# A graph layer on one core: node tiles in offset stages of four, and an output that starts as x + a s

## The chip, the cores and the metric

The kernel runs on one core of a Trainium2 chip. A core has five engines that run side by side and meet through semaphores: PE (matrix products, results in PSUM), DVE (vector), ACT (scalar functions), POOL (general, here it issues gathers) and SP (issues transfers). Sixteen DMA engines move data. The metric is device time in microseconds (us); lower is better. Five runs of the kernel before took 5407.76, 5438.72, 5442.06, 5452.63 and 5453.91 us: the median is 5442.06.

## The reference

There are 12,500 nodes with 160 values each (64 scalars, and 32 vectors of 3) and 400,000 edges, sorted by destination. A node's row is normalized and cut at zero, mapped by four small matrices (two for what is sent along edges, y, and two for what stays, s), and scaled by the node's attribute a. Each edge takes y of its source, multiplies it with weights that a two-layer network makes of the edge's 16 attributes, and adds the result to its destination. The sums z are mapped again and added:

```python
h = jnp.maximum(_layernorm(x, axis=-1), 0.0)
s0 = x0 @ W_sc0 * a * inv0;   y0 = x0 @ W_l1_0 * a * inv0     # x0, x1: the two parts of h
ys0 = y0[edge_src];  ys1 = y1[edge_src]
w = silu(edge_length_embedded @ fc_W1 * ...) @ fc_W2 * ...
z = zeros.at[edge_dst].add(mid) * inv_nb                      # mid: products of w, ys, edge_attr
o0 = z0 @ W_l2_0 * a * inv_mid
out = x + C_S * s + C_X * o
```

## The kernel before, in words

It works in four stages, in the program's order.

Index work (L93 to L152). The edges' destinations are loaded as a 128x3136 table (dst_i). DVE reduces them over windows of three edge tiles (L107), POOL over the partitions (L112), and DVE derives for each group of four windows the first node tile (tile_i), for each edge its row in the window (drel), and one flag, far_i, for edges that no window holds (POOL's second reduction, L151). The temporary tables lie in the pool "idx", which is closed before the node stage. Then the weights are loaded and scaled (L156 to L192), by transfers from ACT's queue.

Node stage (L220 to L256). 98 node tiles of 128 rows, in 14 groups of seven. SP loads a group of x (L217). Per tile: statistics on DVE (L231, L232), one root per group on ACT (L234), normalization on DVE in two pieces (L240, L242), two transposes on PE (L246, L247), the cut at zero on ACT and DVE (L249, L250), two products on PE that give y and s side by side (L252, L253), y times a to yb on ACT (L254), s to acc on DVE (L255). SP stores each group of yb to y_d in HBM (L256). The order of the instructions is left to the framework's scheduler; pools with three or four buffers set how far stages overlap.

Edge loop (L277 to L464), unrolled, with its order written out by hand. 3125 edge tiles of 128 edges, in 782 blocks of four; three blocks make a group. POOL gathers the rows of y_d for each tile (L310), up to eight blocks ahead, into ten buffers yg. PE makes the hidden layer (L319) and the weights (L341), ACT moves the weights out of PSUM (L262, L263: tile wt), DVE multiplies (L268 to L275: tile pr), PE sums the products of a window with a selection matrix (L385), and ACT copies the sums out (L390, L392). Per group PE transposes the sums (L400), maps them (L409) and places them on two node tiles (L421); DVE adds both at once to acc, at an offset from a register that it loads itself (L426, L429). L364 and L366 build the selection from drel on DVE.

After the loop every engine reads far_i (L480) and runs a slow path only if it is set, which it is not here.

Output (L558 to L566). x is loaded again, ACT scales acc by a tile by tile (L562), DVE adds it to x in two pieces, one of them with its columns reordered (L563, L565), and ACT's queue stores (L566).

Of the kernel before, what the change touches and what calls it, by code (L numbers as in the profile page):

```python
# [34 lines left out]
GN = 7  # L35
# [6 lines left out]
def kernel(  # L42
# [45 lines left out]
    nc.vector.memset(eps, EPS)  # L88

# [4 lines left out]
    nc.sync.dma_start(src_sb, src)  # L94
# [3 lines left out]
    far_i = const.tile([P, 1], I32, name="far_i")  # L98
    full = T // WT
    with tc.tile_pool(name="idx", bufs=1) as ip:  # L100
        dst_i = ip.tile([P, TP], I32, name="dst_i")
        nc.sync.dma_start(dst_i, dst)
        nc.vector.tensor_copy(drel, dst_i)
        neg = ip.tile([P, NG * GW], F32, name="neg")
# [6 lines left out]
        negb = ip.tile([P, NG * GW], F32, name="negb")  # L111
        nc.gpsimd.partition_all_reduce(negb, neg, P, bass_isa.ReduceOp.max)  # L112
        first = ip.tile([P, NG], F32, name="first")
# [36 lines left out]
        farb = ip.tile([P, 1], F32, name="farb")  # L150
        nc.gpsimd.partition_all_reduce(farb, far, P, bass_isa.ReduceOp.max)  # L151
        nc.vector.tensor_copy(far_i, farb)  # L152
# [3 lines left out]
    w1 = const.tile([P, 2 * FC_H], F32, name="w1")  # L156
    nc.vector.memset(w1, 0.0)
    for i in range(P // FC_IN):
        nc.scalar.dma_start(w1[FC_IN * i:FC_IN * (i + 1), FC_H * (i % 2):FC_H * (i % 2 + 1)], fc_w1)
    w2 = const.tile([P, NW], F32, name="w2")  # L160
    for i in range(2):
        for to, of, m in ((0, 0, M0), (M0, 2 * M0, M1), (M0 + M1, M0, M0), (2 * M0 + M1, 2 * M0 + M1, M1)):
            nc.scalar.dma_start(w2[FC_H * i:FC_H * (i + 1), to:to + m], fc_w2[:, of:of + m])
    nc.vector.tensor_scalar(w2, w2, 1.0 / math.sqrt(FC_H), None, ALU.mult)

    wn0 = const.tile([M0, 2, M0], F32, name="wn0")
    nc.scalar.dma_start(wn0[:, 0, :], w_l1_0)
    nc.scalar.dma_start(wn0[:, 1, :], w_sc0)
    nc.vector.tensor_scalar(wn0[:, 0, :], wn0[:, 0, :], 1.0 / math.sqrt(M0), None, ALU.mult)
    nc.vector.tensor_scalar(wn0[:, 1, :], wn0[:, 1, :], C_S / math.sqrt(M0), None, ALU.mult)  # L170
    wn1 = const.tile([3 * M1, 2, 3 * M1], F32, name="wn1")
    nc.vector.memset(wn1, 0.0)
    for c in range(3):
        s = slice(M1 * c, M1 * (c + 1))
        nc.scalar.dma_start(wn1[s, 0, s], w_l1_1)
        nc.scalar.dma_start(wn1[s, 1, s], w_sc1)
    nc.vector.tensor_scalar(wn1[:, 0, :], wn1[:, 0, :], 1.0 / math.sqrt(M1), None, ALU.mult)
    nc.vector.tensor_scalar(wn1[:, 1, :], wn1[:, 1, :], C_S / math.sqrt(M1), None, ALU.mult)

    wo = const.tile([P, 3, D], F32, name="wo")  # L180
    nc.vector.memset(wo, 0.0)

    def o1(c):
        return slice(M0 + M1 * c, M0 + M1 * (c + 1))

    nc.scalar.dma_start(wo[0:M0 + M1, 0, 0:M0], w_l2_0)
    for rows, k, c in ((slice(96, P), 0, 0), (slice(0, 32), 1, 1), (slice(32, 64), 1, 2)):
        nc.scalar.dma_start(wo[rows, k, o1(c)], w_l2_1[M0:, :])
    for rows, k, c in ((slice(64, P), 1, 0), (slice(0, 64), 2, 1), (slice(64, P), 2, 2)):
        nc.scalar.dma_start(wo[rows, k, o1(c)], w_l2_1[0:M0, :])  # L190
    nc.vector.tensor_scalar(wo[M0:M0 + M1, 0, 0:M0], wo[M0:M0 + M1, 0, 0:M0], 1.0 / math.sqrt(3.0), None, ALU.mult)
    nc.vector.tensor_scalar(wo, wo, C_X / math.sqrt(10.0 * (M0 + M1)), None, ALU.mult)  # L192
# [3 lines left out]
    nc.sync.dma_start(a_sb, attr)  # L196

# [15 lines left out]
    def load_x(pool, g, n):  # L213
        xt = pool.tile([P, GN, D], F32, name="xt")
        if g + n == NT and N % P:
            nc.vector.memset(xt[:, n - 1, :], 0.0)  # L216
        node_dma(g, n, lambda rows, t, p: nc.sync.dma_start(xt[:p, t, :], by_tile(x[rows, :])))  # L217
        return xt

    with (  # L220
        tc.tile_pool(name="nx", bufs=4) as nx,
        tc.tile_pool(name="nd", bufs=3) as nd,
        tc.tile_pool(name="nd_pt", bufs=3, space=PSUM) as nd_pt,
        tc.tile_pool(name="nd_po", bufs=3, space=PSUM) as nd_po,
    ):
        for g, n in groups:
            xt = load_x(nx, g, n)
            st = nd.tile([P, GN, 6], F32, name="st")
            mv = nd.tile([P, GN, 2], F32, name="mv")
            for j in range(n):  # L230
                nc.vector.bn_stats(st[:, j, :], xt[:, j, :])  # L231
                nc.vector.bn_aggr(mv[:, j, :], st[:, j, :])  # L232
            rstd = nd.tile([P, GN], F32, name="rstd")
            nc.scalar.activation(rstd[:, :n], mv[:, :n, 1], AF.Sqrt, bias=eps)  # L234
            nc.vector.reciprocal(rstd[:, :n], rstd[:, :n])
            yb = nd.tile([P, GN, D], F32, name="yb")
            for j in range(n):
                i = g + j
                h = nd.tile([P, D], F32, name="h")
                nc.vector.tensor_scalar(h[:, 0:M0], xt[:, j, 0:M0], mv[:, j, 0:1], rstd[:, j:j + 1],  # L240
                                        ALU.subtract, ALU.mult)
                nc.vector.tensor_scalar(h[:, M0:].rearrange("p (c u) -> p c u", c=3),  # L242
                                        xt[:, j, M0:].rearrange("p (u c) -> p c u", c=3),
                                        mv[:, j, 0:1], rstd[:, j:j + 1], ALU.subtract, ALU.mult)
                pt = nd_pt.tile([P, 2, P], F32, name="pt")
                nc.tensor.transpose(pt[0:M0, 0, :], h[:, 0:M0], ident)  # L246
                nc.tensor.transpose(pt[0:3 * M1, 1, :], h[:, M0:], ident)  # L247
                hT = nd.tile([P, 2, P], F32, name="hT")
                nc.scalar.activation(hT[0:M0, 0, :], pt[0:M0, 0, :], AF.Relu)  # L249
                nc.vector.tensor_scalar(hT[0:3 * M1, 1, :], pt[0:3 * M1, 1, :], 0.0, None, ALU.max)  # L250
                po = nd_po.tile([P, 2, D], F32, name="po")
                nc.tensor.matmul(po[:, :, 0:M0], hT[0:M0, 0, :], wn0, start=True, stop=True)  # L252
                nc.tensor.matmul(po[:, :, M0:], hT[0:3 * M1, 1, :], wn1, start=True, stop=True)  # L253
                nc.scalar.activation(yb[:, j, :], po[:, 0, :], AF.Copy, scale=a_sb[:, i:i + 1])  # L254
                nc.vector.tensor_copy(acc[:, i, :], po[:, 1, :])  # L255
            node_dma(g, n, lambda rows, t, p: nc.sync.dma_start(by_tile(y_d[rows, :]), yb[:p, t, :]))  # L256
# [8 lines left out]
    def multiply(pr, tmp, wt, yg, ev, n):  # L265
# [8 lines left out]
                             wt[:, :n, M0:96].unsqueeze(2).to_broadcast([P, n, 3, M1]), y1)  # L274
        nc.vector.tensor_mul(pr[:, :n, M0:96], wt[:, :n, 160:NW], tmp[:, :n, 3, :])  # L275

    with (  # L277
        tc.tile_pool(name="ld", bufs=2) as ld,
        tc.tile_pool(name="yg", bufs=10) as ygp,
        tc.tile_pool(name="hid", bufs=4) as hid,  # L280
# [328 lines left out]
```

## Time and profile before

| | us |
|---|---|
| median of five runs | 5442.06 |
| the profiled execution: its time, its span | 5432.29, 5430.4 |
| index work, until x is asked for | 0 to 47.9 |
| node stage, first statistics to last copy into acc | 52.2 to 281.7 |
| first gather, first product of the edge loop | 283.95, 292.2 |
| edge loop ends, output begins | 5377 |
| busy in the span: PE, DVE, ACT, POOL | 3773.9, 2781.8, 2592.3, 3210.4 |

The busy times are sums over stages that have different limits, so they do not tell what bounds any one of them; the stages are read one by one. A wait is given as "engine, tile and line <- releaser: us in total, times, longest", and names what was late last. "issue" and "remote" stand for a releaser that the profile does not tell. The end of a matmul is modelled, not recorded.

### The profile page before, as it was taken

To read this page: it belongs to the slowest core of one execution; us is meant where nothing else is said; L and a number is where in the kernel's file an instruction comes from. 1 tells how busy PE (TensorE), PEld (TensorE's weight loads), DVE (VectorE), ACT (ScalarE), POOL (GpSimd) and SP (SyncE) were. 2 spreads that over 40 slices of the span, in tenths; PEclk is the share of its full clock that TensorE was granted. 3 is DMA by queue.
4 is the path that set the end of the run, shared out by engine and by line. 5 is a ranking of instruction groups with operands and counts; after the bars stand their busy time and mean duration, and the time that the engine had idled before them with its cause. 6 is when DMAs were issued, how large, how long until landed. Compare 5 with 4: busy or idle time off the path is not lost. (4 is left out here: it accounts for less than half of the span.)

```text
span 5430.4 us, 60313 instructions
## 1 busy us (share of the span) xinstructions
PE 3773.9 (69%) x17263; PEld 2663.4 (49%) x17263; DVE 2781.8 (51%) x6412; ACT 2592.3 (48%) x9298; POOL 3210.4 (59%) x3135
## 2 busy tenths in 40 slices
PE   5846777777777676767666777767776776776764
PEld 3534544554555454545444555445554554554543
DVE  6634554544555554555445555545555555555455
ACT  1224454444554454545444445444454544454456
POOL 0065666656666666666566666666666666666661
PEclk9977787877778887878788788887788888888887
DMA  2122222222222222222222222222222222222224
GB/s 84 57 65 55 59 57 57 58 55 58 55 59 61 56 57 57 60 58 58 56 59 57 56 58 57 59 56 57 58 59 59 57 58 60 58 60 58 58 55 134
DMA packets 245943, 327.78 MB, mean 60 GB/s; under 512 B 66040, under 2 KB 195352, under 8 KB 245352
## 3 DMA queue, kind: packets, MB, share of 16 engines
q0 software_dynamic: 150000, 256.20, 17.7%
q1 hardware_dynamic: 81030, 59.43, 3.7%
q10 hardware_dynamic: 14578, 8.25, 0.5%
q8 instruction: 141, 2.31, 0.2%
q14 instruction: 194, 1.59, 0.1%
HBM read 307.62 MB, written 16.00 MB: 60 GB/s over the span
## 5 line engine op out<-in xcount | busy, mean ns | idle before, releaser
L310 POOL DMA_INDIRECT yg<-y_d,src_sb x3125 | 3202.5, 1025 | 2080.8 <-DVE pr L275 956.6
L385 PE MATMUL pz<-pr,sel 128*128 128x256 f32 x6250 | 1877.8, 451 | 218.9 <-issue 128.5
L385 PEld LDWEIGHTS pz<-pr,sel 128*128 128x128 f32 x6250 | 1387.5, 232 | 468.5 <-issue 162.8
L262 ACT ACTIVATE wt<-pw,ev 128x96 f32<-128x96 f32 x3125 | 810.7, 344 | 1184.2 <-issue 995.2
L271 DVE TENSOR_TENSOR pr<-wt,yg 128x256 f32<-128x256 f32 x782 | 329.9, 422 | 1601.9 <-ACT wt L263 1178.3
L390 ACT ACTIVATE zs<-pz 32x192 f32<-32x192 f32 x1042 | 337.8, 324 | 989.8 <-remote 455.3
L341 PE MATMUL pw<-w,hT 64*128 64x192 f32 x6250 | 803.2, 380 | 0.2 <-issue 0.2
L341 PEld LDWEIGHTS pw<-w,hT 64*128 64x128 f32 x6250 | 552.6, 207 | 407.2 <-issue 406.8
L392 ACT ACTIVATE zs<-pz 32x64 f32<-32x64 f32 x3126 | 669.8, 214 | 41.8
L400 PE MATMUL px<-ident,zs 128*128 128x128 f32 (+1 forms) x783 | 215.1, 352 | 516.7 <-ACT zs L390 284.7
L429 DVE TENSOR_TENSOR acc<-acc,px 128x320 f32 x261 | 127.2, 487 | 855.6 <-remote 315.8
L409 PE MATMUL px<-wo,za 128*128 128x160 f32 x1566 | 338.6, 361 | 319.2 <-issue 149.2
L421 PE MATMUL px<-os,place 128*128 128x160 f32 x1044 | 263.6, 385 | 334.9 <-ACT os L411 219.4
L270 DVE TENSOR_REDUCE tmp<-tmp 128x128 f32<-128x384 f32 x782 | 463.8, 593 | 27.0
L409 PEld LDWEIGHTS px<-wo,za 128*128 128x128 f32 x1566 | 264.6, 222 | 390.9 <-issue 187.6
L268 DVE TENSOR_TENSOR tmp<-yg,ev 128x384 f32<-128x384 f32 x782 | 431.6, 552 | 8.6 <-DMA yg<-y_d,src_sb 5.9
L273 DVE TENSOR_TENSOR pr<-wt,yg 128x384 f32<-128x384 f32 x782 | 431.6, 552 | 0.0
L400 PEld LDWEIGHTS px<-ident,zs 128*128 128x128 f32 (+1 forms) x783 | 105.7, 154 | 634.8 <-ACT zs L390 304.8
L319 PE MATMUL px<-xe,w 32*128 32x512 f32 x782 | 316.0, 698 | 128.2 <-issue 84.0
L263 ACT ACTIVATE wt<-pw 128x384 f32<-128x384 f32 x782 | 398.3, 509 | 0.0
L421 PEld LDWEIGHTS px<-os,place 128*128 128x128 f32 x1044 | 186.8, 231 | 411.5 <-ACT os L411 243.5
L366 DVE TENSOR_TENSOR sel<-sel,ev 128x1152 f32<-128x1152 f32 (+1 forms) x261 | 353.7, 1355 | 14.4 <-DMA ev<-in_e 5.4
(78 smaller groups left out, 2025.4 us busy)
## 6 DMA issues: line engine op xcount, KB each, us to landing
yg<-y_d,src_sb POOLq DMA_INDIRECT x3125
xe<-in_e SPq DMA_DIRECT2D x784, 32.0 KB
xt<-in_x SPq DMA_DIRECT2D x26, 560.0 KB
y_d<-yb SPq DMA_DIRECT2D x13, 560.0 KB
out<-xt ACTq DMA_DIRECT2D x13, 560.0 KB
ev<-in_e SPq DMA_DIRECT2D x32, 192.0 KB
src_sb<-in_src SPq DMA_DIRECT2D x1, 1568.0 KB
dst_i<-in_dst SPq DMA_DIRECT2D x1, 1568.0 KB
```

The source lines that it names most:

```text
L262: nc.scalar.activation(wt[:, k, 0:96], pw[:, k, 0:96], AF.Copy, scale=ev[:, k, 0:1])
L263: nc.scalar.activation(wt[:, :n, 96:NW], pw[:, :n, 96:NW], AF.Copy)
L268: nc.vector.tensor_tensor(tmp[:, :n, 0:3, :], y1, ev[:, :n, 1:4].unsqueeze(3).to_broadcast([P, n, 3, M1]), ALU.mult)
L270: nc.vector.tensor_reduce(tmp[:, :n, 3, :], tmp[:, :n, 0:3, :].rearrange("p t c u -> p t u c"), AX.X, ALU.add)
L273: nc.vector.tensor_mul(pr[:, :n, 96:192].rearrange("p t (c u) -> p t c u", c=3), wt[:, :n, M0:96].unsqueeze(2).to_broadcast([P, n, 3, M1]) ...
L310: nc.gpsimd.indirect_dma_start(out=yg[:, k, :], out_offset=None, in_=y_d, in_offset=bass.IndirectOffsetOnAxis(ap=src_sb[:, t:t + 1], axis=0))
L341: nc.tensor.matmul(pw[:, k, 0:NW], hT[r, o:o + P], w2[r, :], start=True, stop=True)
L366: nc.vector.tensor_tensor(sel[:, :n, 0:3, :], sel[:, :n, 3:4, :].to_broadcast([P, n, 3, WN]), ev[:, :n, 1:4].unsqueeze(3).to_broadcast([P, ...
L385: nc.tensor.matmul(pz[:, 0:PC], sels[g][:, t % TG, :, :], pr[:, k, :], start=t % WT == 0, stop=last)
L392: nc.scalar.activation(zs[:, 192 + M0 * c:192 + M0 * (c + 1)], pz[WN * c:WN * (c + 1), 192:PC], AF.Copy)
L409: nc.tensor.matmul(po[:m, :], za[:, k, :m], wo[:, k, :], start=k == 0, stop=k == 2)
L421: nc.tensor.matmul(ps[:, h, :], place[:m, h, :], os[:m, :], start=True, stop=True)
```

## The change

The node stage is cut into parts of four tiles, and its order is written out by hand for PE, ACT, DVE and SP: in one step the statistics and centering of part q, the leaving of part q-3, the maps of part q-2 and the transposes of part q-1. Only the mean is taken off, with the cut at zero, on ACT from x (h); the factor 1/deviation, times a, is the positive number ra and is applied when results leave PSUM. acc starts as x + ra times the mapped row, in the columns' own order, so that weights are laid out for that order instead. x is loaded first, stores of y_d are issued by ACT, the loads of edge weights move to SP, and the index work stands partly after part 6 (first_nodes), partly after the last part (relate). far_i comes from a PE product in place of POOL's second reduction. In the loop the sums are multiplied by a as they are added, in two instructions per group instead of one. The output stage only stores acc, from two queues in turn. Groups have eight tiles. (Lines that stand unchanged in a new function, and removed ones that are printed above, are partly left out.)

```diff
-GN = 7
+GN = 8
+HN = 4
...
+    start = ctx.enter_context(ExitStack())
+    ip = start.enter_context(tc.tile_pool(name="idx", bufs=1))
+    dst_i = ip.tile([P, TP], I32, name="dst_i")
+    neg = ip.tile([P, NG * GW], F32, name="neg")
+    negb = ip.tile([P, NG * GW], F32, name="negb")
+    def first_nodes():
+
         nc.vector.tensor_copy(drel, dst_i)
...
-        negb = ip.tile([P, NG * GW], F32, name="negb")
         nc.gpsimd.partition_all_reduce(negb, neg, P, bass_isa.ReduceOp.max)
+
+    def relate(cnt):
...
-        farb = ip.tile([P, 1], F32, name="farb")
-        nc.gpsimd.partition_all_reduce(farb, far, P, bass_isa.ReduceOp.max)
-        nc.vector.tensor_copy(far_i, farb)
+        nc.tensor.matmul(cnt, far, one, start=True, stop=True)
+        nc.vector.tensor_scalar(far_i, cnt, 1.0, None, ALU.min)
...
+    def node_weights():
+        nc.vector.memset(wnr, 0.0)
...
+        for c in range(3):
+            s = slice(M1 * c, M1 * (c + 1))
+            nc.scalar.dma_start(wnr[c::3, 0, s], w_l1_1)
...
+        nc.vector.tensor_scalar(wn1[:, 0, :], wnr[:, 0, :], 1.0 / math.sqrt(M1), None, ALU.mult)
+        nc.vector.tensor_scalar(wn1[:, 1, :].rearrange("p (u c) -> p c u", c=3),
+                                wnr[:, 1, :].rearrange("p (c u) -> p c u", c=3), C_S / math.sqrt(M1), None, ALU.mult)
...
+    def edge_weight_loads():
+        nc.gpsimd.memset(w1, 0.0)
+        for i in range(P // FC_IN):
+            nc.sync.dma_start(w1[FC_IN * i:FC_IN * (i + 1), FC_H * (i % 2):FC_H * (i % 2 + 1)], fc_w1)
...
+    def edge_weights():
+        nc.vector.tensor_scalar(w2, w2, 1.0 / math.sqrt(FC_H), None, ALU.mult)
...
+        nc.vector.tensor_scalar(wo[:, :, M0:].rearrange("p k (u c) -> p k c u", c=3),
+                                wor[:, :, M0:].rearrange("p k (c u) -> p k c u", c=3), f, None, ALU.mult)
...
-        tc.tile_pool(name="nx", bufs=4) as nx,
-        tc.tile_pool(name="nd", bufs=3) as nd,
-        tc.tile_pool(name="nd_pt", bufs=3, space=PSUM) as nd_pt,
-        tc.tile_pool(name="nd_po", bufs=3, space=PSUM) as nd_po,
+        tc.tile_pool(name="nx", bufs=5) as nx,
+        tc.tile_pool(name="ns", bufs=5) as ns,
+        tc.tile_pool(name="nd", bufs=2) as nd,
+        tc.tile_pool(name="nd_pt", bufs=2, space=PSUM) as nd_pt,
+        tc.tile_pool(name="nd_po", bufs=4, space=PSUM) as nd_po,
...
+        xts, ybs, state = {}, {}, {}
+        parts = [(g, j, min(HN, n - j)) for g, n in groups for j in range(0, n, HN)]
+
+        def load_x(g, n):
+            xt = nx.tile([P, GN, D], F32, name="xt")
+            if g + n == NT and N % P:
+                nc.gpsimd.memset(xt[:, n - 1, :], 0.0)
+            node_dma(g, n, lambda rows, t, p: nc.sync.dma_start(xt[:p, t, :], by_tile(x[rows, :])))
+            xts[g] = xt
+        def center(q):
+
+            g, j, n = parts[q]
...
+                nc.vector.bn_aggr(mv[:, k, :], st[:, k, :])
+            nm = ns.tile([P, HN], F32, name="nm")
+            nc.vector.tensor_scalar(nm[:, :n], mv[:, :n, 0], -1.0, None, ALU.mult)
+            h = nd.tile([P, HN, D], F32, name="h")
+            for k in range(n):
+                nc.scalar.activation(h[:, k, :], xt[:, j + k, :], AF.Relu, bias=nm[:, k:k + 1])
+            ra = ns.tile([P, HN], F32, name="ra")
+            nc.scalar.activation(ra[:, :n], mv[:, :n, 1], AF.Sqrt, bias=eps)
...
+        def turn_rows(q):
+            g, j, n = parts[q]
+            nc.vector.reciprocal(ra[:, :n], ra[:, :n])
+            nc.vector.tensor_mul(ra[:, :n], ra[:, :n], a_sb[:, g + j:g + j + n])
+            pt = nd_pt.tile([P, 2, HN, P], F32, name="pt")
+            for k in range(n):
+                nc.tensor.transpose(pt[0:M0, 0, k, :], h[:, k, 0:M0], ident)
+                nc.tensor.transpose(pt[0:3 * M1, 1, k, :], h[:, k, M0:], ident)
...
+        def map_rows(q):
+            hT = nd.tile([P, 2, HN, P], F32, name="hT")
+            nc.scalar.activation(hT[0:M0, 0, :n, :], pt[0:M0, 0, :n, :], AF.Copy)
+            nc.vector.tensor_copy(hT[0:3 * M1, 1, :n, :], pt[0:3 * M1, 1, :n, :])
+            for k in range(n):
                 po = nd_po.tile([P, 2, D], F32, name="po")
+                nc.tensor.matmul(po[:, :, 0:M0], hT[0:M0, 0, k, :], wn0, start=True, stop=True)
+                nc.tensor.matmul(po[:, :, M0:], hT[0:3 * M1, 1, k, :], wn1, start=True, stop=True)
...
+        def leave(q):
+            for k, po in enumerate(pos):
+                nc.scalar.activation(yb[:, j + k, :], po[:, 0, :], AF.Copy, scale=ra[:, k:k + 1])
+                nc.vector.scalar_tensor_tensor(acc[:, g + j + k, :], po[:, 1, :], ra[:, k:k + 1], xt[:, j + k, :],
+                                               op0=ALU.mult, op1=ALU.add)
+            if q + 1 == len(parts) or parts[q + 1][0] != g:
+                m = j + n
+                node_dma(g, m, lambda rows, t, p: nc.scalar.dma_start(by_tile(y_d[rows, :]), yb[:p, t, :]))
...
+        LEAD = 3
+        with tc.manual_schedule(engines={mybir.EngineType.PE, mybir.EngineType.Activation, mybir.EngineType.DVE,
+                                         mybir.EngineType.SP}):
+            for g, n in groups[:2]:
+                load_x(g, n)
+            nc.sync.dma_start(a_sb, attr)
+            node_weights()
+            nc.sync.dma_start(dst_i, dst)
+            for g, n in groups[2:LEAD]:
+                load_x(g, n)
+            nc.sync.dma_start(src_sb, src)
+            last = len(parts) - 1
+            for q in range(len(parts) + 3):
+                if q <= last and parts[q][1] == 0:
...
+                if q == min(2, last):
+                    edge_weight_loads()
+                if q == min(6, last):
+                    first_nodes()
+                if q <= last:
+                    center(q)
+                if 0 <= q - 3 <= last:
+                    leave(q - 3)
+                if 0 <= q - 2 <= last:
+                    map_rows(q - 2)
+                if 0 <= q - 1 <= last:
+                    turn_rows(q - 1)
+            pt = nd_pt.tile([P, 2, HN, P], F32, name="pt")
+            edge_weights()
+            relate(pt[0:1, 0, 0, 0:1])
+    start.close()
...
+        tc.tile_pool(name="selp", bufs=3) as selp,
+        tc.tile_pool(name="prod", bufs=3) as prod,
...
-            to = acc[:, ds(i, 2), :]
-            nc.vector.tensor_tensor(to, to, ps, ALU.add)
+            for h in range(2):
+                to = acc[:, ds(i + h, 1), :]
+                nc.vector.scalar_tensor_tensor(to, ps[:, h:h + 1, :], a_sb[:, ds(i + h, 1)], to,
+                                               op0=ALU.mult, op1=ALU.add)
...
+    for i, (g, n) in enumerate(groups):
+        eng = (nc.sync, nc.scalar)[i % 2]
+        node_dma(g, n, lambda rows, t, p: eng.dma_start(by_tile(out[rows, :]), acc[:p, g + t.start:g + t.stop, :]))
```

## The prediction

> **What bounds the kernel now.** I read the table of windows by stage first, then the timeline of the seams between stages, then one period of the edge loop, then the waits. The columns of a window are: length, busy us (and instructions) of PE, PEld, DVE, ACT and POOL, granted TensorE clock, share of the DMA engines, GB/s.
>
> ```profile
> 48.00:282.00 234.00, 197.33 (x590) 129.17 (x590) 140.16 (x604) 68.98 (x211) 0.00 (x0) 1.00 0.23 69
> ...
> 308.00:373.00 65.00, 9.80 (x31) 6.74 (x33) 7.90 (x19) 8.50 (x32) 41.29 (x43) 0.50 0.20 54
> 373.00:5340.00 4967.00, 3515.32 (x16390) 2491.78 (x16386) 2541.59 (x5631) 2446.11 (x8832) 3142.54 (x3065) 0.81 0.21 58
> ...
> 5377.00:5430.40 53.40, 0.00 (x0) 0.00 (x0) 20.87 (x30) 32.65 (x98) 0.00 (x0) 0.50 0.99 300
> ```
>
> There are four stages: the index work (0 to 48), the node stage (48 to 282), the edge loop (284 to 5377) and the output (5377 to 5430). The last is bound by the DMA engines (share 0.99), and moved this:
>
> ```profile
> DMA packets 25480, 16.04 MB, mean 303 GB/s; under 512 B 476, under 2 KB 25476, under 8 KB 25476
> ```
>
> The seams, from the timeline (start, length, engine, line):
>
> ```profile
> 47.90 16.94 SPq L217 DMA_DIRECT2D xt<-in_x  x5
> 52.24 0.55 DVE L231 BATCH_NORM_STATS2 st<-xt 128x6 f32<-128x160 f32 x2 [3.90 <-DMA xt<-in_x]
> ...
> 281.40 0.33 DVE L255 COPY acc<-po 128x160 f32<-128x160 f32 x1 [1.33 <-ACT yb L254]
> 283.95 1.30 POOL L310 DMA_INDIRECT yg<-y_d,src_sb  x1 [236.27 <-DMA xe<-in_e]
> 292.17 0.56 DVE L268 TENSOR_TENSOR tmp<-yg,ev 128x384 f32<-128x384 f32 x1 [3.68 <-DMA yg<-y_d,src_sb]
> ```
>
> x is asked for only at 47.90; 98 node tiles then take 229.5 us from the first statistics to the last copy, 2.34 each. One period of the loop:
>
> ```profile
> 1017.02 0.95 POOL L310 DMA_INDIRECT yg<-y_d,src_sb  x1 [0.30 <-issue]
> 1020.47 1.04 ACT L262 ACTIVATE wt<-pw,ev 128x96 f32<-128x96 f32 x4 [5.48 <-issue]
> 1021.92 0.42 DVE L271 TENSOR_TENSOR pr<-wt,yg 128x256 f32<-128x256 f32 x1 [9.94 <-ACT wt L263]
> 1023.07 0.29 DVE L275 TENSOR_TENSOR pr<-wt,tmp 128x128 f32<-128x128 f32 x1
> 1023.42 0.95 POOL L310 DMA_INDIRECT yg<-y_d,src_sb  x1 [5.46 <-DVE pr L275]
> 1023.61 0.49 DVE L429 TENSOR_TENSOR acc<-acc,px 128x320 f32 x1 [0.25 <-PE px L421]
> ```
>
> POOL issues gathers until all ten yg buffers are full, then waits for a product to free one; the product waits for ACT, and ACT for a PE result. The sum into acc (L429) comes after POOL has restarted. Over the loop:
>
> ```profile
> POOL yg L310 <- DVE pr L275: 956.6, 230, 11.1
> ```
>
> The sum into acc, by line (min/median/max ns):
>
> ```profile
> L429 DVEq FUSED_REGOPS  x261: 93/93/104, 375.5 to 5373.9; - x131
> L429 DVE TENSOR_TENSOR acc<-acc,px x261: 480/487/490, 379.1 to 5376.8; 128x320 f32 x131
> ```
>
> **The change, part by part.**
>
> *Start.* x is now first on SP's queue, and its buffers no longer wait for the index work. Before the first statistics DVE scales the node weights: eight ACT-queue issues at the 0.43 to 0.61 us of L167 to L176, some 5 us, and a landing like that of x (47.90 to 52.24, 4.3). PE needs ident, done at 11.48 on POOL. So the pipeline starts near 11.5 instead of 52.2.
>
> *Node period.* A part has four tiles. PE per tile: two transposes that start 0.21 apart (61.49, 61.70 on the timeline), 0.45 for the L252 pair, 0.58 for the L253 pair: 1.45, or 5.8 a part. DVE per part: statistics 4 x 0.29, four sums into acc at the 0.33 of L255, one 96x512 copy 0.6 (four times 128 elements of L250 at 0.285, less three starts), small ones 0.45: 3.5. ACT: four Relus at the 0.33 of L562, a root 0.3, four yb at 0.39, a 64x512 copy at L324's 0.60, half a store issue at 0.37: 4.0. All fit beside PE, but one chain crosses them: transposes 1.7, ACT's copy 0.8 with its signal, DVE's copy 0.7 (it follows ACT's, as L250 followed L249), a signal 0.2, the maps 4.1, less 0.4 for the first map that needs ACT's half alone: 7.1. I take 7.2 and 24.5 parts: 176. Filling (statistics 1.3, Relus 1.3, two table loads at 1.28, transposes 1.7, the next two parts' turns on ACT) costs about 8, draining 2; first_nodes puts L103 and L107 to L110 (5.3) and a 3.3 us POOL reduction, beside which L191 took 1.84, into DVE's order: 5 after slack. Last sum into acc: 11.5 + 8 + 176 + 2 + 5 = 202, against 281.7: **-80**. Ends: PE-bound, 5.8 a part, -114; the old 2.34 per tile, -28.
>
> *Index work behind the maps.* After the last tile DVE does edge_weights (about 1.8, from L164 and L192) and relate: 1.2 + 6 x 0.3 + 1.25 + 4 x 0.145 + 4 x 0.44 + 2 x 0.70 + 3.55 + 3.5 + 3.4 + 3.4 = 21.9, 1 for the count through PE, 1.9 for the first selection: 26.6 to the first product, where it was 10.4 (281.73 to 292.17). On PE the count stands before the first weigh, so ACT's first wt waits behind it too. It is 16 us late, but gathers need only the stores and the last tile, and POOL ran from 283.95 to 360.7 without waiting for anyone while PE did 31 matmuls in 65 us. Ends 0 and +16; nearest to the first, since POOL carries that stretch: **+5**.
>
> *Sums into acc.* 261 times one 128x320 sum (487 ns) becomes two 128x160 ones (0.33 each, L255), with four register steps (93 ns) instead of one. Exposed wholly: 2 x 0.33 - 0.40 (the spacing of L429 to the next) + 3 x 0.093 = 0.54, or +141. Hidden wholly: 0; a gain is excluded, as nothing is removed from DVE. DVE is busy half the loop, and the sum follows POOL's restart; behind it stands only the next block's L268, whose product waits for ACT in most periods. Nearest to 0: **+10**.
>
> *Output.* No x loads, scaling or adds: 8.0 MB where 16.04 MB took 53.4 us, so 26.7 at the same rate plus 2 for the first issue and last landing: **-25**. Ends: -30 (at 363 GB/s, the best slice), -14 (at the 209 of a poor slice). It is also issued from two queues. [...]
>
> *At nothing.* Fourteen y_d stores on ACT's queue (5.2) lie in ACT's idle 3 us per part. Twenty-three small loads on SP (about 10) stand before an x group that is wanted several parts later. The reordered pools put DVE-written tiles over the index area, so xe and gathers wait for the last tile, not for relate.
>
> Sum: -80 + 5 + 10 - 25 = **-90**. The profiled execution took 5432.3 (span 5430.4), 9.8 under the median: 5342 there, 5352 against the median.
>
> The clock: at 0.50 while PE starves (308 to 373), at 1.00 in the node stage. [...]
>
> **The rivals.**
> - *The node chain keeps its length.* For it: PE is marked busy 197 of the node stage's 234 us, 2.0 a tile, and my 1.45 takes the spacings of dense stretches alone (61.5 to 68 on the timeline). Against it: each wait between engines now serves four tiles. Then -28 + 5 + 10 - 25 = -38: 5404.
> - *DVE's added work is on the loop's path.* For it: when gathers are over, DVE works nearly without a gap, 10.2 to 10.7 us a group. Against it: 19.5 us a group while they flow. Fully exposed, -100 + 141 = +41: 5483, slower. It breaks even at 0.38 us a group.
> - *The loop takes another rhythm.* POOL's 956.6 us of waits depend on how far PE gets between full buffers; a tenth less with a late consumer gives 5256, a tenth more 5448.
> - *The index work is not hidden*, +16: 5363, within the likeliest range.
>
> **How the numbers follow.** Likeliest (node chain near 7.2, loop as before): 0.62, 5315 to 5395. Node chain unchanged 0.10; DVE exposed by half or more 0.13 (5415 to 5490); a better rhythm 0.07; a worse one 0.08 (5400 to 5450). The five runs differ by 0.8%, and 0.5% is about what can be told from no change. Faster: 0.62 + 0.10 + 0.07 + 0.02 of the last two; within 0.5% (5415 to 5469): 0.10; slower: 0.09. Leaving out the ends, 5300 to 5430.
>
> **What would show it.** Right: x issued before 2 us, the first gather near 205, PE waiting in the node stage mostly before the maps, a last stage of about 28 us at a DMA share near 1, a loop of 19.5 us a group. Wrong: a part that takes over 8 us, a gather that waits for the index work, POOL waiting well over 956.6 us, or the output not halved.

## The result, and the profile after

The changed kernel is slightly slower: 5480.0 us (median of 39 runs, 5425.66 to 5511.28) against 5443.8 us (median of 65 runs of the kernel before), a ratio of 1.0059 with a 95% interval of 1.0045 to 1.0073. The forecast was 5352. The profiled execution took 5495.9 us, its span is 5494.1. It is 16 us above its median, and the profiled execution of before was 11.5 us under the median of the 65, so the two spans stand 64 us apart where the medians stand 36 apart. Some 28 us of what the two traces differ by is scatter.

The changed kernel's table of windows by stage, with the columns of the table in the prediction:

```profile
11.50:303.40 291.90, 206.43 (x588) 134.45 (x588) 102.11 (x388) 81.17 (x246) 3.92 (x3) 1.00 0.19 59
303.40:330.20 26.80, 6.05 (x24) 3.59 (x24) 25.90 (x36) 4.00 (x10) 20.53 (x14) 1.00 0.28 77
330.20:5464.50 5134.30, 3623.14 (x16655) 2548.02 (x16655) 2655.37 (x5996) 2482.48 (x8981) 3175.59 (x3112) 0.80 0.21 57
5464.50:5494.10 29.60, 0.00 (x0) 0.00 (x0) 0.00 (x0) 0.00 (x0) 0.00 (x0) 0.53 0.93 271
```

The node stage now starts at 11.5, 40 us earlier than before, but ends at 303.4, 22 us later: it has grown from 229.5 to 292 us. Its clock of 1.00 in this table (and in the prediction's) is not a measurement: the trace's first clock record comes at 336 us (before: 291), and a stretch without records is printed as 1.00, as 0 to 48 us before, where PE does nothing. What the clock was is taken up with the form of the maps. The index work follows (DVE is busy for 25.9 of 26.8 us while POOL already gathers). From the first gather (305.71) to the last sum (5464.5) the loop takes 5159 us, where it took 5093 (283.95 to 5377). The output takes 29.6 us in place of 53.4. With the first gather 22 later: 22 + 66 - 24 = 64, the distance between the two spans. The output did what it should, as the DMA view of that last window shows:

```profile
DMA packets 12724, 8.03 MB, mean 271 GB/s; under 512 B 222, under 2 KB 12722, under 8 KB 12722
```

Half of the bytes, and still bound by the DMA engines (share 0.93). So there are two things to explain: the node stage, and the loop.

**A part of the node stage.** The timeline of the changed kernel, from the end of one part's maps to the next part's (start, length, engine, line; in brackets the idle time before, and what ended it):

```profile
156.62 1.01 PE L288 MATMUL po<-wn,hT 96*128 96x192 f32 x2
157.41 0.42 PE L274 MATMUL pt<-ident,h 128*64 128x128 f32 x1
...
158.91 0.42 PE L275 MATMUL pt<-ident,h 128*96 128x128 f32 x1
159.37 1.38 ACT L262 ACTIVATE h<-xt,nm 128x160 f32<-128x160 f32 x4 [8.51 <-PE pt L275]
160.66 0.28 ACT L264 ACTIVATE ra<-mv,eps 128x4 f32<-128x4 f32 x1
160.84 1.21 ACT L299 ACTIVATE yb<-po,ra 128x160 f32<-128x160 f32 x4
...
162.50 0.59 ACT L282 ACTIVATE hT<-pt 64x512 f32<-64x512 f32 x1 [0.44 <-ACT yb L299]
...
163.14 0.79 PE L287 MATMUL po<-wn,hT 64*128 64x128 f32 x2 [3.81 <-ACT hT L282]
...
171.13 0.42 PE L275 MATMUL pt<-ident,h 128*96 128x128 f32 x1
171.59 1.38 ACT L262 ACTIVATE h<-xt,nm 128x160 f32<-128x160 f32 x4 [8.50 <-PE pt L275]
```

Read it as a ring. ACT's four Relus (L262) start only when PE has finished the transposes (L275), because there are two buffers for h, and the one that the Relus write is still being read. Then come root, yb and the copy of hT on ACT, and only then PE's maps, and behind them the next transposes. PE and ACT take turns: 12.2 us for this part (159.37 to 171.59), 11.7 for the ones in which ACT doesn't also issue a store of y, 12.0 in the mean. The table of waits has it as its largest entry of that stage:

```profile
ACT h L262 <- PE pt L275: 188.2, 22, 9.5
```

**The loop.** POOL's waits for a product went from 956.6 us to 1015.8, which is most of the loop's growth in this pair of executions (in another execution of the changed kernel, beside 5328 us below, they were 870.1, so this total scatters):

```profile
POOL yg L393 <- DVE pr L358: 1015.8, 231, 8.5
```

And this is a sum into acc on the changed kernel's timeline, with the next block's first operation:

```profile
1011.81 0.80 DVE L513 SCALAR_TENSOR_TENSOR acc<-px,a_sb,acc 128x160 f32 x2 [3.07 <-PE px L504]
1012.53 0.60 DVE L351 TENSOR_TENSOR tmp<-yg,ev 128x384 f32<-128x384 f32 x1
```

The same place in the kernel before:

```profile
999.92 0.49 DVE L429 TENSOR_TENSOR acc<-acc,px 128x320 f32 x1 [1.19 <-PE px L421]
1000.32 0.55 DVE L268 TENSOR_TENSOR tmp<-yg,ev 128x384 f32<-128x384 f32 x1
```

The next operation starts 0.72 us behind the sum's start instead of 0.40: 0.32 us of DVE per group, 82 us over 261 groups if it were all exposed. The three more register steps come to nothing on top: in the trace two of the four run under the first of the two sums (at 1011.82 and 1011.95), the other two well before it, beside a product.

### The profile page after: what moved, and what is told of

The parts are those of the page before. It is cut to its first block, busy times and chain, and to the rows that moved or that the text cites. A ratio compares the mean times of both kernels' runs of the same rounds, so it can differ in the third digit from the quotient of the medians.

```text
span 5494.1 us, 61160 instructions
## 1 busy us (share of the span) xinstructions
PE 3835.6 (70%) x17265; PEld 2686.1 (49%) x17265; DVE 2786.8 (51%) x6435; ACT 2569.5 (47%) x9237; POOL 3201.4 (58%) x3137
## 3 DMA queue, kind: packets, MB, share of 16 engines
q14 instruction: 200, 1.64, 0.1%
## 5 line engine op out<-in xcount | busy, mean ns | idle before, releaser
L393 POOL DMA_INDIRECT yg<-y_d,src_sb x3125 | 3196.1, 1023 | 2012.9 <-DVE pr L358 1015.8
L424 PE MATMUL pw<-w,hT 64*128 64x192 f32 x6250 | 818.1, 386 | 3.5 <-DVE far_i L159 3.3
L424 PEld LDWEIGHTS pw<-w,hT 64*128 64x128 f32 x6250 | 564.1, 211 | 430.7 <-issue 429.6
L513 DVE SCALAR_TENSOR_TENSOR acc<-px,a_sb,acc 128x160 f32 x522 | 200.3, 384 | 857.8 <-PE px L504 311.3
L402 PE MATMUL px<-xe,w 32*128 32x512 f32 x782 | 370.9, 735 | 227.5 <-issue 104.6
```

Source lines behind the costliest of these rows:

```text
L393: nc.gpsimd.indirect_dma_start(out=yg[:, k, :], out_offset=None, in_=y_d, in_offset=bass.IndirectOffsetOnAxis(ap=src_sb[:, t:t + 1], axis=0))
L402: nc.tensor.matmul(ph, w1[r, :], xe[r, :], start=True, stop=True)
L424: nc.tensor.matmul(pw[:, k, 0:NW], hT[r, o:o + P], w2[r, :], start=True, stop=True)
```

## The experiments

Theory: (1) the node stage is bound by a ring through PE and ACT, closed by the two h buffers; (2) the loop pays for part of the split sum. Rivals: the node stage is bound by PE alone; the loop is longer for what lies around it (the late index work, the changed places of tiles in memory). The runs fell on several chips, and the kernel before took 5336 us beside the first four, 4517 beside the next four, and 5328 and 5449 beside the last two sets. So every result is a ratio to runs of the kernel before taken beside it; it is not the plain quotient of the two medians and can differ from that by about 0.001.

### The node stage: buffers, order on PE, form of the maps

**A third buffer for h.**

```diff
+        tc.tile_pool(name="nh", bufs=3) as nh,
...
-            h = nd.tile([P, HN, D], F32, name="h")
+            h = nh.tile([P, HN, D], F32, name="h")
```

> The changed kernel with three buffers for h in place of two (the Relus' target), nothing else. Theory (ring): ACT's Relus of a part wait for the last transposes of two parts before, which stand last on PE, behind the maps; then follow 1.4 of Relus, 0.3 root, 1.2 of yb, 0.6 of hT copy, 6.5 of maps and 1.9 of transposes, 12.2 us a part, as traced. With a third buffer Relus, root and yb run beside the maps and the ring is hT copy, maps and transposes: about 9.3 a part; the last sum into acc comes near 235 to 245 instead of 303, the first gather as much earlier, and the time falls by 55 to 65 us, to about 5420. Rival (PE or the loads set the part): the period stays above 11.5 and the time within 15 us of the changed kernel's 5480.

Measured: 5313.8 us, ratio 0.9952 (0.9922 to 0.9982), 22 us faster than before, where the changed kernel is 36 to 43 slower. The first gather came at 246.7 instead of 305.7. The timeline of this kernel:

```profile
149.56 0.59 ACT L283 ACTIVATE hT<-pt 64x512 f32<-64x512 f32 x1 [1.31 <-PE pt L276]
...
150.20 0.79 PE L288 MATMUL po<-wn,hT 64*128 64x128 f32 x2 [0.68 <-ACT hT L283]
...
153.12 1.38 ACT L263 ACTIVATE h<-xt,nm 128x160 f32<-128x160 f32 x4 [2.97 <-DVE nm L260]
...
158.65 0.59 ACT L283 ACTIVATE hT<-pt 64x512 f32<-64x512 f32 x1 [1.31 <-PE pt L276]
```

The Relus now wait for DVE's statistics and run beside the maps; PE waits 0.68 us instead of 3.81 before a part's maps, and a part takes 9.1 us (149.56 to 158.65) instead of 12.2. The theory had 9.3. The ring is shown, and it was 59 us of the node stage.

**Transposes ahead of maps**, with the third buffer:

```diff
-                if 0 <= q - 2 <= last:
-                    map_rows(q - 2)
                 if 0 <= q - 1 <= last:
                     turn_rows(q - 1)
+                if 0 <= q - 2 <= last:
+                    map_rows(q - 2)
```

> The changed kernel with three buffers for h and, on PE, the transposes of a part ahead of the maps of the part before it. Theory (ring): ACT's copy of hT then runs beside the transposes, and PE is bound by its own 1.9 + 6.6 = 8.5 us a part; with three buffers alone it was 9.1 and the first gather came at 246.7. First gather near 232, ratio to before 0.992 (the three buffers alone: 0.9952). Rival (the reduced ring has moved to another wait): first gather at 245 or later, ratio 0.995.

Measured: first gather at 228.0, where 232 was expected. Ratio 0.9856 (0.9841 to 0.9871), better than the 0.992 expected; but this set ran beside a kernel before of 4517 us, in which gathers run back to back, and there added DVE work turned out to cost next to nothing (below). The place of the first gather decides: the node stage is now bound by PE, which is busy for 196 of 200 us and waits once for ACT's copy (3.9 us):

```profile
20.00:220.00 200.00, 196.00 (x560) 128.46 (x560) 98.07 (x357) 78.40 (x226) 3.56 (x2) 0.50 0.23 66
```

**The form of the maps.** That left the maps themselves: 6.6 us a part, where the prediction had 4.1. They stand by turns on the changed kernel's timeline, one of 64 rows, one of 96:

```profile
150.91 0.79 PE L287 MATMUL po<-wn,hT 64*128 64x128 f32 x2 [3.26 <-ACT hT L282]
151.64 1.01 PE L288 MATMUL po<-wn,hT 96*128 96x192 f32 x2
152.57 0.79 PE L287 MATMUL po<-wn,hT 64*128 64x128 f32 x2
153.30 1.01 PE L288 MATMUL po<-wn,hT 96*128 96x192 f32 x2
```

A tile's two maps take 1.66 us (150.91 to 152.57). The kernel before, where it had three tiles ready at once:

```profile
62.91 1.65 PE L252 MATMUL po<-wn,hT 64*128 64x128 f32 x6
64.48 2.29 PE L253 MATMUL po<-wn,hT 96*128 96x192 f32 x6
66.56 0.42 PE L246 MATMUL pt<-ident,h 128*64 128x128 f32 x1
```

The same three pairs take 3.65 us, 1.22 a tile, because they stand grouped by form: one turn from 64 to 96 rows instead of five turns. Grouping them in the changed kernel, alone, and with the two repairs above and the one of the index work below:

```diff
                 nc.tensor.matmul(po[:, :, 0:M0], hT[0:M0, 0, k, :], wn0, start=True, stop=True)
-                nc.tensor.matmul(po[:, :, M0:], hT[0:3 * M1, 1, k, :], wn1, start=True, stop=True)
                 pos.append(po)
+            for k, po in enumerate(pos):
+                nc.tensor.matmul(po[:, :, M0:], hT[0:3 * M1, 1, k, :], wn1, start=True, stop=True)
```

> The changed kernel with the maps of a part grouped on PE: the four 64-row ones, then the four 96-row ones, in place of one of each by turns; nothing else. In the trace of before, maps of one form that stand in a row start 0.43 (64 rows) and 0.49 to 0.64 (96 rows) apart; by turns, as in the changed kernel, a pair takes 1.65, 6.6 a part. Theory (the turns between the two forms cost the difference): about 4.4 a part and a period of 10.0 instead of 12.2, first gather near 252 instead of 305.7, ratio to before 0.996 to 0.998 in a loop paced by late PE results, 0.989 with gathers back to back. Rival (a map takes 1.65 in any order once four tiles share a wait): first gather at 300 or later.

Measured alone: ratio 0.9984 (0.9957 to 1.0010), first gather at 260.0 instead of 305.7. A part's eight maps on its timeline:

```profile
153.26 2.07 PE L287 MATMUL po<-wn,hT 64*128 64x128 f32 x8 [3.26 <-ACT hT L282]
155.26 2.93 PE L290 MATMUL po<-wn,hT 96*128 96x192 f32 x8
157.98 0.42 PE L274 MATMUL pt<-ident,h 128*64 128x128 f32 x1
```

4.7 us from the first map to the first transpose instead of 6.5 (150.91 to 157.41). The rival, that a map costs the same in any order, has fallen; 4.4 was expected, the first gather came 8 us later than the 252 expected, and the ratio a little above the 0.996 to 0.998 expected. The turns are what costs: a grouped part has six fewer of them, and its way from the first map to the first transpose is 1.78 us shorter (4.72 against 6.50), 0.30 a turn. What happens in a turn, no run here shows.

The clock is not the cause of this gain. The kernel with three h buffers and transposes first has clock records in its node stage, 0.50 from 19 to 258 us, and there a part's maps, by turns, take 6.18 us from the first start to the last: exactly what they take in the changed kernel, which so very likely ran its whole node stage at half clock too. Grouped, the same takes 4.40 at a recorded 0.50 (49 to 240 us of the kernel with grouped maps alone), so the gain from grouping stands at one and the same clock. Where the kernel below that has all repairs records 1.00 (98 to 108 us), the grouped maps take 2.3:

```profile
99.51 1.16 PE L296 MATMUL po<-wn,hT 64*128 64x128 f32 x8 [1.02 <-DVE ra L279]
100.59 1.57 PE L299 MATMUL po<-wn,hT 96*128 96x192 f32 x8
```

No run has maps by turns at a recorded full clock, and why the clock stays low beside a PE that is busy is not shown.

> The changed kernel with three buffers for h, transposes ahead of maps, index work in pieces, and the maps of a part grouped by form. Theory: PE's part is 1.9 + 4.4 = 6.3, the first gather comes between 182 and 192 instead of 228; ratio to before 0.983 to 0.986 in a loop paced by late PE results (0.9919 without the grouping), 0.974 to 0.976 with gathers back to back (0.9835). Rival (another engine or the four po buffers take over as the bound): first gather past 205.

Measured with all: 5357.8 us against 5448.6 beside it, ratio 0.9824 (0.9793 to 0.9855), first gather at 186.2. Three causes of the long node stage add up to 119.5 us: the third buffer 59, the order on PE 19, the grouping 42 (the pieces of index work leave the first gather where it was). The time is then 91 us under before, as much as the forecast, but by other terms: the first gather is 98 earlier where 80 was forecast, and the loop pays more than 15.

### The loop: what the split sum costs

**One sum in the changed kernel, two in the kernel before, two plain ones.** The first edit, in the changed kernel; its reverse is the second run's, in the kernel before:

```diff
-            for h in range(2):
-                to = acc[:, ds(i + h, 1), :]
-                nc.vector.scalar_tensor_tensor(to, ps[:, h:h + 1, :], a_sb[:, ds(i + h, 1)], to,
-                                               op0=ALU.mult, op1=ALU.add)
+            to = acc[:, ds(i, 2), :]
+            nc.vector.tensor_tensor(to, to, ps, ALU.add)
```

The third, in the changed kernel:

```diff
-                nc.vector.scalar_tensor_tensor(to, ps[:, h:h + 1, :], a_sb[:, ds(i + h, 1)], to,
-                                               op0=ALU.mult, op1=ALU.add)
+                nc.vector.tensor_tensor(to, to, ps[:, h:h + 1, :], ALU.add)
```

> The changed kernel with one 128x320 addition per group in place of the two scaled 128x160 ones; the node attribute is left out of the sums. Theory (the split sum is exposed): from the first gather to the last 5046 us as before the change, where the changed kernel took 5113, and the time falls by 50 to 65 us, to about 5420. Rival (the loop is longer for what lies around it: the late index work, the tiles' places in memory, the stores of y): 5095 or more from first to last gather, and the time within 15 us of 5480.

> The kernel before with the two scaled 128x160 sums in place of its one 128x320 addition, nothing else; the node attribute is then applied twice to the sums. Theory (the split sum is exposed): first to last gather goes from 5046 to some 5100 to 5115, the time from 5444 to about 5500, slower by 1.0 to 1.2%. Rival (the loop is longer for what lies around it): 5046 within 15, time 5444 within 15.

> The changed kernel with two plain 128x160 additions per group: the sum stays split, but without the scaling operand and its register steps; the node attribute is left out of the sums. If the cost is DVE's time in the two halves (2 x 0.33 and their register steps against 2 x 0.38 and four), most of it stays: the time is 10 to 25 us under 5480. If it is the scaled form with its extra register steps alone, the time falls to about 5420, as with one addition.

Measured, all beside the same 5335.6 us: one sum in the changed kernel 1.0000 (0.9972 to 1.0028); two scaled ones in the kernel before 1.0031 (1.0000 to 1.0062); two plain ones in the changed kernel 1.0076 (1.0048 to 1.0105). The directions fit, the sizes fall between theory and rival: the single sum gains some 31 us on the changed kernel's 1.0059, where 50 to 65 was expected, and the split costs the kernel before 17 us (0 to 33), where 55 was expected. Two plain sums, where 10 to 25 us less was expected, gain nothing, so it is the split that costs, and not the scaled form: against one sum they are 35 us slower (some 20 to 60 by the intervals), though DVE's next operation starts only 0.19 us later than behind one (0.59 against 0.40, the median), 49 us in all. In single profiles the effect can't be seen: the four kernels of this set, the one with three h buffers among them, took 4974 to 4988 us from first to last gather. The expectation of 5046 against 5113 took the scatter between two executions for a part of the cost.

**The same difference with the node stage repaired** (third buffer, order on PE, index work in pieces), beside the changed kernel itself and one more run of added DVE work:

> The changed kernel as it is, beside the three that follow. Two paces of the edge loop have been seen: PE's results seen late and POOL waiting for products (some 860 to 1016 us of waits, 1.59 to 1.64 us per gather), and gathers back to back (1.335 us per gather, no such wait). In the first, if the split sum costs something there, ratio to before 1.004 to 1.007 and 35 us more than the same kernel's front and output alone explain (+22 and -25); in the second, where added DVE work was hidden, 0.999 to 1.001.

> The changed kernel with three buffers for h, transposes ahead of maps and the index work in pieces, once more. With gathers back to back 0.9835 as before. In a loop paced by late PE results: first gather at 229, 55 us earlier than before, output 25 us shorter, and the loop longer by the split sum's 20 to 45: ratio 0.991 to 0.994.

> The kernel of the third row with one plain 128x320 addition per group in place of the two scaled ones; the node attribute is left out of the sums. The difference to the third row is the split sum's price: 20 to 45 us in a loop paced by late PE results (ratio to before 0.985), under 5 with gathers back to back (0.983). Rival (the split costs nothing anywhere): within 10 us of the third row in both.

(The third row is the repaired kernel with the split sum.)

Measured, all beside 5328.0 us: the changed kernel 1.0077 (1.0052 to 1.0102); repaired, with the split sum, 5283.9 us, 0.9919 (0.9896 to 0.9942); repaired, with one sum, 5247.8 us, 0.9856 (0.9826 to 0.9886). The last two differ by 36 us; the intervals make it some 14 to 54. That is the split sum's price here, some 45% of the 82 us of DVE that it adds (17 to 66%). It also answers the rival of the loop: with one sum, the earlier first gather (-55) and the shorter output (-24) make -79, and -80 was measured (-93 to -61), so nothing beyond the interval is left for the changed places of tiles in memory.

**DVE work without a PE result.** Does a split sum cost by DVE's time, or by holding a PE result (px) longer? The kernel before, with four more additions behind each sum:

```diff
             nc.vector.tensor_tensor(to, to, ps, ALU.add)
+            for k in range(4):
+                nc.vector.tensor_tensor(work, work, iota[:, 0:160], ALU.add)
```

> The kernel before with four more 128x160 additions on DVE behind each group's sum, on a tile of their own: no PE result is read or held longer, and no register steps are added. They add some 4 x 0.3 = 1.2 us of DVE time per group, 315 us in all. Theory (DVE's time in that place is partly exposed, as the split sum's was: some 20 to 45 us of its 141): the same share of 15 to 30%, 45 to 95 us, ratio to before 1.008 to 1.018. Rival (the split costs because a PE result is held longer, or by its register steps): within 15 us of before, ratio 0.997 to 1.003. Rival (DVE is the bound): over 200 us, ratio over 1.037.

> The kernel before with four more 128x160 additions on DVE per group on a tile of their own, once more. With gathers back to back it cost 6 us of the 315 added. In a loop paced by late PE results: 45 to 95 us (1.008 to 1.018) if DVE's time in that place is exposed there as the split sum's seemed to be; within 15 us of before if the split sum costs by holding a PE result longer or not at all.

The two runs gave different answers: ratio 1.0014 (1.0005 to 1.0023), 7 us, beside a kernel before of 4517 us; and 1.0135 (1.0110 to 1.0161), 70 us, beside one of 5328. The additions push the next block's first operation back by 1.3 us a group, 342 us in all, so a fifth of them (17 to 25%) is exposed in the slow loop, with no PE result held. DVE's time in that place does cost, then; but a fifth of the split sum's 82 us is 17, at the low end of its 14 to 54, and the price does not follow DVE's time from run to run: 35 us for 49 (two plain sums), 36 for 82 (two scaled ones), 70 for 342 (four additions). Whether the rest is scatter or the PE result px that is held longer is not shown.

Why the two differ is seen in the repaired kernel with the split sum, which ran in both sets (1.34 and 1.59 us from gather to gather). In the set of 4517 us, by the table of costliest groups:

```profile
L407 POOL DMA_INDIRECT yg<-y_d,src_sb x3125 | 3220.1, 1030 | 1024.6 <-issue 918.8 <-DMA xe<-in_e 72.9 <-DMA yg<-y_d,src_sb 11.6
...
L359 ACT ACTIVATE wt<-pw,ev 128x96 f32<-128x96 f32 x3125 | 810.9, 344 | 329.0 <-ACT zs L489 203.8 <-issue 59.7 <-PE pw L438 54.6
```

In the set of 5328 us:

```profile
L407 POOL DMA_INDIRECT yg<-y_d,src_sb x3125 | 3208.9, 1027 | 1829.5 <-DVE pr L372 858.4 <-issue 837.9 <-DMA xe<-in_e 72.9
...
L359 ACT ACTIVATE wt<-pw,ev 128x96 f32<-128x96 f32 x3125 | 810.7, 343 | 1119.1 <-issue 973.1 <-ACT zs L489 44.1 <-PE pz L482 35.3
```

The gathers themselves take the same time. In the first set POOL hardly waits for a product (4.9 us in all): it is the bound, a gather every 1.34 us, and DVE work disappears beside it. In the second ACT's weighing waits 973 us in which the profile shows nothing that it waits for, products come late, and POOL waits for them; whatever lengthens the work between two full sets of yg buffers is then partly on the path. That PE's work is there and its completion is seen late is a reading, since the ends of matmuls are modelled. In the period of the kernel before that the prediction shows, PE's products pw

```profile
1017.05 1.65 PE L341 MATMUL pw<-w,hT 64*128 64x192 f32 x8
```

end at 1018.70, and ACT, which needs them, starts at 1020.47.

### The index work, and the output

**Index work in pieces during the node stage**, one piece a part (`relate` becomes a generator with a `yield` behind each piece, and what was its last step becomes `count_far`):

```diff
                     center(q)
+                if q >= min(9, last):
+                    far = next(steps, far)
...
             edge_weights()
-            relate(pt[0:1, 0, 0, 0:1])
+            count_far(pt[0:1, 0, 0, 0:1], far)
```

> The changed kernel with the second half of the index work done in pieces during the node stage, one piece a part, in DVE's idle time before the sums into acc; h keeps its two buffers. First product near 312 instead of 330, part period 12.2 as before. Theory (the late index work costs some 7 us, since POOL carries the loop's first 60 us): ratio to before 1.0045, where the changed kernel has 1.0059. If it costs its full 16 us, 1.003; if the loop's slower pace follows from the late start, 1.000 or less.

> The changed kernel with all three: three buffers for h, transposes ahead of maps, index work in pieces during the node stage. If the repairs add up: first gather near 235, first product 10 us behind it, ratio to before 0.990 to 0.992, and what is left of the forecast -90 us is the split sum's cost in the loop. Rival (DVE becomes the bound of the node stage with the pieces of 3.4 us in it): first gather past 245, ratio 0.994 or more.

Measured beside 4517.4 us: in the changed kernel 1.0010 (1.0001 to 1.0019), first product (here the first pr) at 314.0 instead of 330.1, first gather unchanged at 305.7. No run of the changed kernel itself stands beside it, so this ratio says nothing of the index work alone. The repaired kernel does: with the late index work 4451.6 us (0.9856), with the pieces 4441.3 us (0.9835; 0.9822 to 0.9849), first product at 237.2 instead of 252.4. The 15 us cost 10 of them where gathers run back to back (1 to 18 by the intervals). What they cost in the slow loop was not measured by itself; in the trace of the changed kernel its gather number 125 is 7 us later, counted from the first, than in the trace of before, and 3 us later in the changed kernel's other trace.

**The sums kept plain and x read again at the end**, everything else repaired. acc holds the unscaled sum, and out = x + a acc is formed in the last stage, half of the tiles by ACT's scaling and one wide addition, half by a scaled addition on DVE. The first of its edits:

```diff
-                nc.vector.scalar_tensor_tensor(acc[:, g + j + k, :], po[:, 1, :], ra[:, k:k + 1], xt[:, j + k, :],
-                                               op0=ALU.mult, op1=ALU.add)
+                nc.vector.tensor_scalar(acc[:, g + j + k, :], po[:, 1, :], rs[:, k:k + 1], None, ALU.mult)
```

> The kernel of the second row, but acc keeps the sums unscaled and without x, as before the change: one plain 128x320 addition per group, and x read again, scaled and added at the end. Theory: the last stage is 23 to 27 us longer again, and the sums are 36 us cheaper in a loop paced by late PE results, where the ratio becomes 0.980 to 0.984, a little under the second row's; with gathers back to back, where the split sum was hidden, it is 23 to 27 us over the second row, 0.979 to 0.982.

(The second row is the kernel with all repairs and grouped maps.)

Measured: 5348.5 us, 0.9806 (0.9775 to 0.9838), against 5357.8 with the split sum and the short output. Its last stage, from the table of windows:

```profile
5280.60:5333.50 52.90, 0.00 (x0) 0.00 (x0) 24.84 (x63) 16.38 (x49) 0.23 (x1) 0.51 1.01 303
```

The stage is 23 us longer than the changed kernel's 29.6, as expected, and the whole is 9 us faster; the intervals overlap, so no gain of storing x + a s is seen in a slow loop, and one of up to some 15 us is not excluded. It is the fastest version of its set, 100 us under the kernel before.

## Why the prediction was wrong

- **Start: right.** x was asked for at 0.74 and the first transpose ran at 11.55; the prediction had 11.5.
- **Node period, the step that failed.** Forecast 7.2 us a part, measured 12.0, beyond the 8 that the prediction itself named as a sign of being wrong (21 parts from 27.1 to 278.9 on ACT's Relus): 4.8 x 21 = 101, and the last sum came at 303.4 instead of 202. Two terms were wrong. The maps were priced at 1.03 a tile, by spacings inside runs of one form and so without any turn, less than even the grouped stretch of before gives by its starts (1.22), and the changed order takes the forms by turns, at 1.66: 6.5 a part from the first map to the first transpose, 2.4 more than forecast. And the chain from transposes to maps left out Relus, root and yb, 2.7 a part (159.37 to 162.05), because ACT's work was only checked against PE's total (4.0 of 7.2) and not against the buffers that it writes: with two h buffers, and the transposes last on PE, the Relus can't start before PE is done. Every second part adds ACT's store issue, 0.4; the copies cost 0.65 instead of 1.3. Transposes 1.9, Relus, root and yb 2.7, store 0.2, copies 0.65 and maps 6.5 make the 12.0.
- **The lower end was no bound.** The old 2.34 us per tile was taken as the worst that could happen; a new order can be worse than the one that it replaces, and was: 2.98.
- **The clock was misread.** The prediction has it at 1.00 in the node stage, where the trace has no clock record; by the starts of the maps it was most likely 0.50 all along. The old spacings, from which its prices come, are of the same clock, so this did not put the sum wrong. A PE that is marked busy did not mean a clock of 1.00: the kernel with three h buffers and transposes first has PE marked busy for 196 of 200 us, and its recorded clock stayed at 0.50.
- **Sums into acc: right in kind, too small.** +10 forecast, about +36 measured (14 to 54). Full exposure was put too high, at 141: the register steps run beside other work, and 82 is what the trace gives. The argument that the sum follows POOL's restart holds for one restart; that the delay is passed on to the next block's product, for which POOL waits again, is the likely step that it left out, but no run shows it.
- **Index work: near in size.** 25 us from the last sum to the first product, 26.6 forecast. Its price was forecast at +5; it was 10 of 15 us (1 to 18) where it could be priced, which is not the loop of the forecast.
- **Output: right.** -25 forecast, -24 measured, DMA share 0.93; the two queues moved 271 GB/s together, where loads and stores moved 303 before.
- **Sum.** 22 (first gather) + 7 (index work, from one pair of traces) + 36 (split sum) - 24 (output) = +41, against +36 between the medians and +43 in the later set. The forecast of -90 lost 102 on the first gather and 26 on the sums. The rival with a slower result, DVE fully on the path, gave nearly the measured time (5483) for a reason that the runs refute: most of the loss lay in the node stage, which that rival had at the forecast's -80.

## What to carry to other kernels

When work is regrouped in offset stages, write the order of every engine down for one period and follow each buffer around: an engine's total that fits the period says nothing if a buffer makes two engines take turns (here ACT's 4.0 fitted 7.2, and a part took 12.0). Take a matmul's price from a stretch with the same neighbours, since the turn between two shapes cost 0.30 us here, where 64-row maps that follow each other start 0.43 apart. And an end of a range that is "as slow as before" is no bound for an order that did not exist before.

## What the runs showed of the hardware

One program's loop has two paces: 1.34 us a gather with POOL hardly waiting for a product, and 1.58 to 1.64 with 830 to 1016 us of such waits, ACT's unexplained idle time before its weighing at 52 to 60 us in the one and 852 to 1104 in the other. The kernel before took 4517 us in the first and 5328 to 5449 in the second. All runs of one set shared a pace, whichever kernel they ran, so it belongs to where or when a program runs. The fast pace was seen in one set alone; two sets on another chip than that one's took 5328 and 5449, both in the slow pace, so whether the chip fixes it is open. The granted clock differs as well, between 400 us and the end of the loop 0.91 to 0.92 in the one and 0.80 to 0.82 in the other; whether that is a cause or follows from a PE that waits was not tested. Why ACT sees PE's results late in the one and not in the other was not found. A price measured in a loop of one pace doesn't hold in the other: 342 us of DVE work cost 7 us in the fast one and 70 in the slow one.

A printed clock of 1.00 can mean that there is no clock record, as up to 291 us in the kernel before and up to 336 in the changed one. Here the maps tell the clock where the records don't: a part's maps take, from the first start to the last, 6.18 us by turns at 0.50, and grouped 4.40 at 0.50 and 2.3 at 1.00.
